# Gate and up weights loaded in blocks of 32 by 32 and turned on VectorE

## The chip, the core and the metric

One core of one Trainium2 chip. The metric is the device time of one execution in microseconds; the kernel before took 1469.0 us, the median of 3 runs (1468.91 to 1469.15). A core has TensorE (PE, matrix products; PEld is its weight load), VectorE (DVE), ScalarE (ACT), GpSimd (POOL) and SyncE (SP, which only issues transfers here). Each engine works through its own instructions in order.

## The reference

A gated block of cross-attention and a gated feed-forward network, all in f32: x is 4 x 1024 x 512, ctx 4 x 64 x 512, 16 heads of 64. The three weights of the feed-forward part are first rounded to 4-bit levels in blocks of 32 along their inner dimension; activations are rounded to 16-bit levels with one scale for a whole tensor. Cut to what the change touches:

```
def lpbq_dequant(w):                      # w is O x I
    wb = w.reshape(O, I // 32, 32)
    s  = max(max(|wb|, axis=-1) / 7, 1e-12)
    return (clip(round(wb / s), -8, 7) * s).reshape(O, I)

x    = act_qdq(layernorm(x))                           # 16-bit levels, one scale
up   = act_qdq(x @ lpbq_dequant(w_up).T)               # w_up:   1536 x 512
gate = act_qdq(x @ lpbq_dequant(w_gate).T)             # w_gate: 1536 x 512
gate = act_qdq(gate * fixed_qdq_u16(sigmoid(gate)))
out  = act_qdq(gate * up) @ lpbq_dequant(w_down).T     # w_down: 512 x 1536
```

The two products contract over the 512 inputs, and TensorE contracts over partitions. So gate's and up's weights are wanted with the inputs on partitions, while in DRAM a row is one output, and the blocks of 32 lie along the row.

## The kernel before

The stages follow each other: preparation of the attention's matrices (to about 80 us of the span); attention, a loop over 16 pairs of token tiles (L735, q is the pair, one iteration about 28 us); the gate stage from 561 us, 24 units (the loop at L981), each of 7 products of blocks in the manner of Strassen, 4 matmuls of 128x512 each; the up stage with 24 such units; and the down stage. PE's order is written out by hand (manual_schedule, L818 for the gate and up stages); the other engines are ordered by a planner that goes by priorities, except where keep_in_program_order or high_priority says otherwise.

The 512 inputs are HC = 4 groups of 128. A weight of 1536 outputs is IC = 12 chunks of 128 rows. One chunk goes through these steps:

- `dequantized` (L216): one load of 256 KB on SP's queue (L218), 128 rows of 2 KB. On DVE the largest magnitude of each block (L221), its scale (L224) and reciprocal (L226), the product rounded to int16 (L229), and the product with the scale (L230).
- `turned_chunk` (L243) and `turned` (L232): four PE transposes of 128x128 into PSUM (L235), and one ACT copy of 128x512 out of it (L237) into wgT or wuT. Those hold four chunks each, with inputs on partitions.

`slot()` gives the large buffers, 20 in turn of 128 x 2048 f32 each; a load into a slot waits for what last used it.

Where it stands: in attention, iterations q = 1 to 12 load and round one gate chunk each (`made_ready`, L790), chunks 4 to 11 first, then 0 to 3. The groups 4 to 7 and 8 to 11 are stored by POOL as rows in wg_d (L793), since the slots are needed, and come back at q = 13 and 14 (L800). At q = 13, 14 and 15 PE turns four chunks each ahead of the attention's last product (L769). At q = 13 and 14 the first four chunks of up are loaded and rounded too (`early_up`); PE turns them in the tail of attention (L808, L811). The rest of up, chunks 4 to 11, is loaded and rounded in units 0 to 7 of the gate stage and turned one unit later (L981 to L998). From unit 8 the 12 chunks of the down weight are rounded, one a unit; they are turned later by PE as well (`down_turned`, L264, which stays). `weight_sums` (L279) makes the sums of weight blocks that the seven products need, on DVE: two for gate at the end of attention, the other in the first unit, and those of up from unit 12.

Lines that the prediction speaks of: in attention, scores L570, maximum L594 and L604, exponentials L606, the normalisation L611 and L612, transposes of the weights L627, the product with the values L661, its addition to the tokens (xg) L669; the normalised tokens L692 (xm), their transposes L700 and copies L702; sums over a batch's matrices L381 to L386; loads of token groups L302 and of batch matrices (mb, vb) L710. In the units: the matmul L839 and the copy out of PSUM L855 (raw_gate).

Of the kernel before, what the change touches and what calls it, by code (L numbers as in the profile page):

```python
# [7 lines left out]
F32 = mybir.dt.float32  # L8
I16 = mybir.dt.int16
# [3 lines left out]
ALU = mybir.AluOpType  # L13
AX = mybir.AxisListType
PSUM = bass.MemoryType.PSUM
DRAM = bass.MemoryType.DRAM

P = 128
# [9 lines left out]
def kernel(  # L28
# [40 lines left out]
    nc = tc.nc  # L69
    B, S, H = x.shape  # L70
# [5 lines left out]
    T = B * S  # L76
    NT = T // P
    TPB = S // P
    HC = H // P
    HP = NH // 2  # L80
    IC = I // P
# [7 lines left out]
    QB = 32  # L89
    NQB = H // QB  # L90
# [8 lines left out]
    BL = 32  # L99
    UPE = 4  # L100
    SOON = 150
    NQ = NT // 2
# [6 lines left out]
    dram = ctx.enter_context(tc.tile_pool(name="dram", bufs=1, space=DRAM))  # L109
    big = ctx.enter_context(tc.tile_pool(name="big", bufs=NS))  # L110

    def slot(shape, name, dtype=F32):

        return big.tile(shape, dtype, name=name, tag="s8")
# [6 lines left out]
        out=cmask, in_=cmask, compare_op=ALU.is_ge, fill=-10000.0, base=0,  # L121
# [27 lines left out]
    off2 = const.tile([P, NT], F32, name="off2")  # L149

    x1_d = [dram.tile([P, H], F32, name=f"x1_d{t}") for t in range(NT)]
    wg_d = [dram.tile([P, 4, H], F32, name=f"wg_d{k}") for k in range(2)]
    xh_d = [dram.tile([P, HC, TB], F32, name=f"xh_d{g}") for g in range(NG - 2)]
    m_d, vwo_d = (
        {b: [dram.tile([P, HC, H], F32, name=f"{n}_d{b}_{k}") for k in range(2)] for b in range(2, B)}
# [57 lines left out]
            nc.vector.tensor_scalar(inv, inv, unit, None, ALU.mult)  # L213
        return s, inv

    def dequantized(pool, src, w, name, in_order=False):  # L216

        nc.sync.dma_start(out=w, in_=src)  # L218
        wb = w.rearrange("p (n k) -> p n k", k=QB)
        am = pool.tile([P, NQB], F32, name=f"wam_{name}", tag="wam")  # L220
        ins = nc.vector.tensor_reduce(am, wb, AX.X, ALU.max, apply_absolute_value=True)  # L221
        if in_order:
            tc.keep_in_program_order(ins)
        nc.vector.tensor_scalar(am, am, 1.0 / W_QMAX, 1e-12, ALU.mult, ALU.max)  # L224
        inv = pool.tile([P, NQB], F32, name=f"winv_{name}", tag="winv")
        nc.vector.reciprocal(inv, am)  # L226
        shape = [P, NQB, QB]
        wi = pool.tile(shape, I16, name=f"wi_{name}", tag="wi", bufs=1)
        nc.vector.tensor_tensor(wi, wb, inv.unsqueeze(2).to_broadcast(shape), ALU.mult)  # L229
        nc.vector.tensor_tensor(wb, wi, am.unsqueeze(2).to_broadcast(shape), ALU.mult)  # L230

    def turned(ps, w, dst):  # L232

        for j in range(4):
            nc.tensor.transpose(ps[:, j, :], w[:, j * P : (j + 1) * P], ident)  # L235
        with tc.high_priority(SOON):
            nc.scalar.copy(dst, ps)  # L237

    wgT, wuT, wd, wdT, up_chunks = [], [], [], [], []

    def turned_chunk(psp, w, oc, into, name):  # L243

        if oc % 4 == 0:
            into.append(slot([P, HC, 4 * P], f"w{name}T{oc // 4}"))
        cols = slice((oc % 4) * P, (oc % 4 + 1) * P)
        ps = psp.tile([P, 4, P], F32, name=f"wps_{name}{oc}", tag="tr")
        turned(ps, w, into[-1][:, :, cols])

    def up_chunk(psp, w):
        oc = len(up_chunks)
        up_chunks.append(oc)
        turned_chunk(psp, w, oc, wuT, "u")

    def down_chunk(pool, k):
        if k % 4 == 0:
# [70 lines left out]
    pa = pools.enter_context(tc.tile_pool(name="pa", bufs=2))  # L328
# [222 lines left out]
    with tc.tile_pool(name="ps_s", bufs=1, space=PSUM) as ps_s, tc.tile_pool(  # L551
# [157 lines left out]
                parts[k] = slot([P, HC, H], f"{name}_{k}")  # L709
                nc.sync.dma_start(out=parts[k], in_=src[k])  # L710

        sg_t, ag, early_up, gate_raw = [], [], [], []
        last = NT - GRP
        norm_of(pa, first_norm(*range(1, 5)), "a1")

# [1 line left out]
            if q < NQ:  # L717
                left[q] = score_left(q, two)

        def made_ready(ws, n, src, name, first=0, in_order=False):  # L720

            oc = (len(ws) + first) % n
            if oc % 4 == 0:
                made_in.append(slot([P, min(4, n - oc), H], f"w_{name}{oc}"))
            w = made_in[-1][:, oc % 4, :]
            dequantized(pa, src[oc * P : (oc + 1) * P, :], w, f"{name}{oc}", in_order)
            ws.append(w)

        made_in = []
        two = centred(1)  # L730
        ahead = scores(0, {3: lambda: next_left(1)})
        softmax(0, ahead)
# [2 lines left out]
        for q in range(NQ):  # L735
# [28 lines left out]
            if q % 2 == 1 and q // 2 + 2 < NG:  # L764
                load_group(q // 2 + 2)
                if q // 2 + 2 > 4:
                    group_stats(pa, q // 2 + 2, xg[q // 2 + 2])

            j = q - (NQ - IC // 4)  # L769
            if j >= 0:  # L770
                for oc in range(4 * j, 4 * j + 4):
                    turned_chunk(ps_tr, gate_raw[oc], oc, wgT, "g")
            if q + 1 == NQ:
                for p in range(UPB - 2):
                    ag.append(weight_sums(wgT, sg_t, p, "g"))
# [12 lines left out]
                norm_of(pa, parts, f"b{g}")  # L788

            if 0 < q <= IC:  # L790
                made_ready(gate_raw, IC, w_gate, "g", 4, q < 4)
                if q % 4 == 0 and q < IC:
                    nc.gpsimd.dma_start(out=wg_d[q // 4 - 1], in_=made_in[-1])  # L793
                if q == IC:
                    gate_raw = [*gate_raw[-4:], *gate_raw[:-4]]
            elif q > IC:
                k = q - IC - 1
                if k < 2:
                    w4 = slot([P, 4, H], f"wg_{k}")
                    nc.sync.dma_start(out=w4, in_=wg_d[k])  # L800
                    gate_raw[4 * k + 4 : 4 * k + 8] = [w4[:, i, :] for i in range(4)]
                for _ in range(2 if k < 2 else 0):
                    made_ready(early_up, UPE, w_up, "eu")
        renormed(last)
        renormed(last + 1)
        norm_of(pa, [second_norm(slice(last + 2, NT))], "c2")
        for w in early_up[:-1]:
            up_chunk(ps_tr, w)  # L808
        renormed(NT - 2)
        renormed(NT - 1)  # L810
        up_chunk(ps_tr, early_up[-1])  # L811
    pools.close()

    s_x, inv_x = act_scale(over_all([am_x], "x"), None, "x")

    with tc.tile_pool(name="praw", bufs=RAW) as praw, tc.tile_pool(
# [79 lines left out]


        au, su_t = [], []
        with tc.tile_pool(name="pb", bufs=2) as pb, tc.tile_pool(
            name="ps_tr2", bufs=2, space=PSUM  # L900
        ) as ps_tr:
            def on_dve(tb, h):
                v = xT[tb][:, h, :]
                nc.vector.tensor_scalar(v, v, inv_x, MAGIC, ALU.mult, ALU.add)
# [71 lines left out]


            pairs = [NTB // 2 - 1, *range(NTB // 2 - 1)]
            w4 = [slot([P, 4, H], "w_u4")]
            ready = []  # L980
            for at, v in enumerate(tp * UPB + p for tp in pairs for p in range(UPB)):  # L981
                if at % UPB == 0:
                    b = token_side(v // UPB)
                    for p in range(len(ag), UPB):
                        ag.append(weight_sums(wgT, sg_t, p, "g"))
                    if at + UPB < NV:
                        load_normed(pairs[at // UPB + 1])
                interleaved(unit_steps(v, ag[v % UPB], b, "gate", gate_sum, gate_done))
                if at < IC - UPE:
                    oc = UPE + at  # L990
                    if at == 4:
                        w4.append(slot([P, 4, H], "w_u8"))
                    w = w4[-1][:, at % 4, :]
                    dequantized(pb, w_up[oc * P : (oc + 1) * P, :], w, f"u{oc}")
                    ready.append(w)
                if len(ready) > 1 or at >= IC - UPE and ready:
                    up_chunk(ps_tr, ready.pop(0))
                if at >= IC - UPE and at - (IC - UPE) < IC:  # L998
                    down_chunk(pb, at - (IC - UPE))
                if 0 <= at - IC < UPB:  # L1000
                    au.append(weight_sums(wuT, su_t, at - IC, "u"))
# [503 lines left out]
```

## Time and profile before

| | |
|---|---|
| runs shown, median | 1469.0 us |
| profiled execution, its own time | 1467.07 us |
| its span (first to last instruction) | 1465.3 us |
| PE's granted clock over the span | 0.995 |
| L235 transposes of gate and up | 96, 273 ns each at the median |
| L237 copies of wgT | 12, 6.2 us, 620 ns each |
| L237 copies of wuT | 12, 6.9 us, 594 ns each |
| L221, L229, L230 of gate, one chunk | 667, 686 and 685 ns |
| transposes on DVE (L396, 128x32) | 1, 211 ns |
| chunk loads (L218) of gate | 12, median 427 ns on SP |

One execution is profiled, on its own, so a sum made from its rows is compared with its own 1467.07 us. The runs shown lie 1.9 us above it. Busy time of an engine counts its instructions; short ones overlap in part, so the place that a row of them takes on its engine is read from the start of the first to the start of what follows.

### The profile page before, as it was taken

How to read it: one execution, taken by the hardware profiler on the slowest of the kernel's cores; microseconds unless marked ns; L12 is line 12 of the kernel's file. 1: busy time of each engine (PE TensorE's matmuls, PEld its weight loads, DVE VectorE, ACT ScalarE, POOL GpSimd, SP SyncE). 2: the span in 40 equal slices, each digit the busy share in tenths (PEclk: the TensorE clock that was granted, in tenths of full speed). 3: DMA queues.
4: the chain of work that ended last, by engine and by line, in shares of the span. 5: the costliest groups of instructions: out<-in, count | busy, mean ns of one | idle time of the engine just before them, and what ended most of it. 6: DMA issues, size and time to landing. Idle time of an engine off the chain costs nothing. (4 is left out here: it accounts for less than half of the span.)

```text
span 1465.3 us, 15463 instructions
## 1 busy us (share of the span) xinstructions
PE 1417.2 (97%) x5040; PEld 869.3 (59%) x5040; DVE 1128.0 (77%) x2059; ACT 693.4 (47%) x1746; POOL 96.6 (7%) x191
## 2 busy tenths in 40 slices
PE   8898999999999998999999999999999899999999
PEld 6545766766676674444444444444444448888887
DVE  2976887977988779899956569988888897666632
ACT  2645867767678673111000049977776532222200
POOL 0100000000000001000000000000000101111110
PEclk9999999999999999999999999999999999999999
DMA  9630231431312133664322439958557475554321
GB/s 330 244 130 15 72 115 72 159 129 58 130 47 110 46 130 158 236 223 187 129 86 102 157 127 345 373 216 316 212 210 267 164 282 174 187 187 172 143 72 43
DMA packets 74168, 240.12 MB, mean 164 GB/s; under 512 B 7396, under 2 KB 7652, under 8 KB 68068
## 3 DMA queue, kind: packets, MB, share of 16 engines
q1 hardware_dynamic: 48612, 137.39, 26.8%
q0 software_dynamic: 18560, 76.56, 13.4%
q10 hardware_dynamic: 6912, 25.17, 4.3%
q8 instruction: 39, 0.64, 0.2%
q14 instruction: 45, 0.37, 0.1%
HBM read 130.03 MB, written 109.05 MB: 163 GB/s over the span
## 5 line engine op out<-in xcount | busy, mean ns | idle before, releaser
L606 ACT ACTIVATE e<-e,mx 128x64 f32<-128x64 f32 x480 | 159.7, 339 | 2.2 <-DVE mx L604 2.1
L839 PE MATMUL pqup<-t,wuT 128*128 128x512 f32 x192 | 92.3, 603 | 5.2 <-DVE raw_up L860 2.6
L606 ACT ACTIVATION_READ_ACCUMULATOR e<-e,mx 128x1 f32 x480 | 92.3, 192 | 0.0
L839 PE MATMUL pqgate<-t,wgT 128*128 128x512 f32 x192 | 90.2, 592 | 0.0
L855 ACT COPY raw_gate<-ppgate 128x512 f32<-128x512 f32 x24 | 14.0, 585 | 145.5 <-PE ppgate L839 145.5
L1372 PE MATMUL ep<-wdT,upe 128*128 128x256 f32 x336 | 77.1, 379 | 0.0
L1298 ACT ACTIVATE uie<-upe,inv_up 128x1024 int16<-128x1024 f32 x48 | 53.8, 1145 | 45.8 <-DVE upe L1302 28.7
L661 PE MATMUL oq<-t,eT 128*128 128x256 f32 x256 | 63.7, 393 | 12.0 <-DVE xg L669 8.1
L1372 PE MATMUL eq<-tw,upe 128*128 128x256 f32 x312 | 72.4, 379 | 0.0
L1372 PEld LDWEIGHTS ep<-wdT,upe 128*128 128x128 f32 x336 | 63.8, 190 | 9.1 <-issue 0.5
L1071 ACT ACTIVATE gi<-gt,inv_gate 128x1024 int16<-128x1024 f32 x48 | 54.9, 1143 | 30.3 <-DVE q L1081 30.0
L839 PEld LDWEIGHTS pqup<-t,wuT 128*128 128x128 f32 x192 | 34.7, 189 | 57.0 <-issue 29.7
L839 PE MATMUL ppgate<-xh,wgT 128*128 128x512 f32 x144 | 67.7, 592 | 0.0
L839 PE MATMUL ppup<-xu,wuT 128*128 128x512 f32 x144 | 67.7, 592 | 0.0
L1372 PEld LDWEIGHTS eq<-tw,upe 128*128 128x128 f32 x312 | 59.3, 190 | 8.1
L839 PEld LDWEIGHTS pqgate<-t,wgT 128*128 128x128 f32 x192 | 36.3, 190 | 46.1 <-issue 37.9
L1302 DVE SCALAR_TENSOR_TENSOR upe<-uie,inv_o,gse 128x1024 f32<-128x1024 int16 (+1 forms) x50 | 60.4, 1231 | 3.3 <-ACT uie L1298 3.0
L661 PEld LDWEIGHTS oq<-t,eT 128*128 128x128 f32 x256 | 49.4, 195 | 21.9 <-DVE xg L669 11.0
L570 PE MATMUL sq<-t,xs 128*128 128x512 f32 x128 | 60.3, 593 | 0.0
L629 ACT COPY eT<-ps_e 128x512 f32<-128x512 f32 x64 | 34.3, 588 | 53.5 <-PE ps_e L627 53.5
L967 DVE TENSOR_REDUCE am_gate<-raw_gate 128x1 f32<-128x1024 f32 x48 | 58.2, 1213 | 0.9
L1103 ACT ACTIVATE ar<-raw_up 128x1024 f32<-128x1024 f32 x46 | 48.2, 1047 | 19.1 <-DVE raw_up L1029 19.1
(353 smaller groups left out, 3141.2 us busy)
## 6 DMA issues: line engine op xcount, KB each, us to landing
gate_d<-raw_gate ACTq DMA_DIRECT2D x48, 512.0 KB, 2.6
gt<-gate_d SPq DMA_DIRECT2D x48, 512.0 KB, 4.8
upe<-up_d SPq DMA_DIRECT2D x24, 1024.0 KB, 5.9
up_d<-raw_up POOLq DMA_DIRECT2D x46, 512.0 KB, 3.5
gse<-gsi_d SPq DMA_DIRECT2D x24, 512.0 KB, 4.6
gsi_d<-q SPq DMA_DIRECT2D x44, 256.0 KB, 4.0
xg<-in_x_dram SPq DMA_DIRECT2D x8, 1024.0 KB, 5.2
x_d<-xg POOLq DMA_DIRECT2D x32, 256.0 KB, 2.3
```

The costliest lines, as they stand in the source:

```text
L570: nc.tensor.matmul(bank[at], a[k][:, h, :], b[k][:, h, :], start=start and h == 0, stop=h == HC // 2 - 1, skip_group_check=True,)
L606: nc.scalar.activation(ei[:, h, :], ei[:, h, :], AF.Exp, bias=mx[:, h : h + 1], accum_out=sm[:, h : h + 1],)
L629: nc.scalar.copy(eT[:, 2 * i + k], ps)
L661: nc.tensor.matmul(bank[at], a[k][:, h, :], b[k][:, h, :], start=start and h == 0, stop=h == HP // 2 - 1, skip_group_check=True,)
L839: nc.tensor.matmul(bank[at], a[k][:, h, :], b[k][:, h, :], start=start and h == 0, stop=h == HC // 2 - 1, skip_group_check=True,)
L855: nc.scalar.copy(r0[:, 0, :], bank["pp"])
L967: nc.vector.tensor_reduce(am_gate[:, u : u + 1], rf, AX.X, ALU.max, apply_absolute_value=True)
L1071: nc.scalar.activation(gi, g, AF.Copy, scale=inv_g)
L1103: nc.scalar.activation(ar, raw[u], AF.Abs)
L1298: nc.scalar.activation(ui, up[:, i, :], AF.Copy, scale=inv_u)
L1302: ins = nc.vector.scalar_tensor_tensor(o[:, i, w], ui[:, w], c_o, gs[:, i, w], ALU.mult, ALU.mult)
L1372: nc.tensor.matmul(bank[at], a[u // 2][k][:, u % 2, q % 2, :], w_of[u // 2][k][:, u % 2, :], start=start and u == 0, stop=u == UPB - 1, sk ...
```

## The change

A chunk of gate or up is loaded straight into its place in wgT or wuT, by 16 loads: one for each 32 inputs within a group (a) and each group of inputs (c). Each writes 32 partitions with 4 x 32 elements, in pieces of 32 elements (128 bytes). Partition a·32 + o then holds outputs, column block b holds 32 inputs a·32 to a·32 + 31 of output b·32 + o. Blocks of 32 still lie along a row, so the rounding (`levels`) works on it as before, in a view of four dimensions. Then one DVE transpose in place turns each 32 by 32 block, which puts inputs on partitions and outputs along the row. No PE transposes and no ACT copies are left for gate and up; the down weight keeps them.

wg_d keeps turned groups, and both come back at q = 13. Up's chunks 0 to 3 are made at q = 13 and 14 as before; its chunks 4 to 11 are made in units 2 to 9 of the gate stage (before: 0 to 7), with their first instruction kept in program order. The PSUM buffers of the gate stage's transposes (ps_tr2) go.

```diff
-    wg_d = [dram.tile([P, 4, H], F32, name=f"wg_d{k}") for k in range(2)]
+    wg_d = [dram.tile([P, HC, 4 * P], F32, name=f"wg_d{k}") for k in range(2)]
...
-    def turned_chunk(psp, w, oc, into, name):
+    def turned_chunk(pool, src, oc, into, name, in_order=False):
         if oc % 4 == 0:
-            into.append(slot([P, HC, 4 * P], f"w{name}T{oc // 4}"))
-        cols = slice((oc % 4) * P, (oc % 4 + 1) * P)
-        ps = psp.tile([P, 4, P], F32, name=f"wps_{name}{oc}", tag="tr")
-        turned(ps, w, into[-1][:, :, cols])
+            into[oc // 4] = slot([P, HC, 4 * P], f"w{name}T{oc // 4}")
+        w = into[oc // 4][:, :, (oc % 4) * P : (oc % 4 + 1) * P]
+        blocks = w.rearrange("p c (b k) -> p c b k", k=BL)
+        rows = src[oc * P : (oc + 1) * P, :].rearrange("(b o) (c a k) -> a o c b k", o=BL, k=BL, c=HC)
+        for a in range(P // BL):
+            for c in range(HC):
+                nc.sync.dma_start(out=blocks[a * BL : (a + 1) * BL, c], in_=rows[a, :, c])
+        levels(pool, blocks, [P, HC, P // BL, QB], f"{name}{oc}", in_order)
+        nc.vector.transpose(w, w)
...
-            j = q - (NQ - IC // 4)
-            if j >= 0:
-                for oc in range(4 * j, 4 * j + 4):
-                    turned_chunk(ps_tr, gate_raw[oc], oc, wgT, "g")
...
             if 0 < q <= IC:
-                made_ready(gate_raw, IC, w_gate, "g", 4, q < 4)
-                if q % 4 == 0 and q < IC:
-                    nc.gpsimd.dma_start(out=wg_d[q // 4 - 1], in_=made_in[-1])
+                oc = (q + 3) % IC
+                turned_chunk(pa, w_gate, oc, wgT, "g", q < 4)
+                if oc > 3 and oc % 4 == 3:
+                    nc.gpsimd.dma_start(out=wg_d[oc // 4 - 1], in_=wgT[oc // 4])
...
             elif q > IC:
...
+                for j in (1, 2) if k == 1 else ():
+                    wgT[j] = slot([P, HC, 4 * P], f"wgTb{j}")
+                    nc.sync.dma_start(out=wgT[j], in_=wg_d[j - 1])
+                if k < 3:
+                    for oc in range(2 * k - 2, 2 * k):
+                        turned_chunk(pa, w_up, oc, wuT, "u")
...
-        for w in early_up[:-1]:
-            up_chunk(ps_tr, w)
         renormed(NT - 2)
         renormed(NT - 1)
-        up_chunk(ps_tr, early_up[-1])
...
-                if at < IC - UPE:
-                    oc = UPE + at
...
-                    dequantized(pb, w_up[oc * P : (oc + 1) * P, :], w, f"u{oc}")
-                    ready.append(w)
-                if len(ready) > 1 or at >= IC - UPE and ready:
-                    up_chunk(ps_tr, ready.pop(0))
+                if 1 < at < IC - UPE + 2:
+                    oc = UPE + at - 2
+                    turned_chunk(pb, w_up, oc, wuT, "u", True)
```

`levels` is the DVE part of the old `dequantized`, with the shape handed in:

```diff
+    def levels(pool, w, shape, name, in_order=False):
...
+        ins = nc.vector.tensor_reduce(am_b, w, AX.X, ALU.max, apply_absolute_value=True)
...
+        nc.vector.tensor_tensor(wi, w, inv_b.unsqueeze(len(shape) - 1).to_broadcast(shape), ALU.mult)
+        nc.vector.tensor_tensor(w, wi, am_b.unsqueeze(len(shape) - 1).to_broadcast(shape), ALU.mult)
```

## The prediction

> **What bounds the kernel now.** The first part of the page says which engine is full, the second where.
>
> ```profile
> PE 1417.2 (97%) x5040; PEld 869.3 (59%) x5040; DVE 1128.0 (77%) x2059; ACT 693.4 (47%) x1746; POOL 96.6 (7%) x191
> ...
> PE   8898999999999998999999999999999899999999
> ...
> DVE  2976887977988779899956569988888897666632
> ...
> PEclk9999999999999999999999999999999999999999
> DMA  9630231431312133664322439958557475554321
> ```
>
> The reader is to see that TensorE (PE) is at nine tenths in nearly every slice at full clock, so an instruction taken off PE is worth its place on PE, unless another engine then keeps PE waiting. The engine to suspect is VectorE (DVE): 77% over the span, nine tenths in slices 17 to 20. One slice is 36.6 us; the edit lies in slices 3 to 19. So the second view is that of stretches of 50 us (columns: window; its length; busy PE, PEld, DVE, ACT, POOL with instructions; clock; DMA share; GB/s).
>
> ```profile
> 450.00:500.00 50.00, 49.68 (x223) 35.27 (x222) 35.96 (x76) 39.26 (x154) 1.61 (x3) 1.00 0.14 53
> 500.00:550.00 50.00, 48.32 (x233) 36.98 (x232) 41.18 (x100) 33.00 (x111) 2.16 (x4) 1.00 0.30 106
> 550.00:600.00 50.00, 44.62 (x134) 22.78 (x133) 48.71 (x109) 13.06 (x24) 5.73 (x11) 0.97 0.47 177
> 600.00:650.00 50.00, 50.00 (x130) 22.89 (x129) 40.02 (x76) 7.03 (x12) 2.12 (x4) 1.00 0.70 253
> 650.00:700.00 50.00, 50.00 (x124) 22.51 (x123) 49.73 (x107) 5.85 (x10) 2.28 (x4) 1.00 0.41 158
> ```
>
> Attention ends near 551; from 561 the gate stage runs. In 600 to 700 PE has no gap, though DVE is full in the second half: the gate stage is PE's, with a DVE that just keeps up. From 550 to 600 PE loses 5.4 us, and DVE has 1.3 us free there: the turn between the stages is DVE's. The third view, PE's timeline, shows what the removed transposes really hold (start, length, instructions, idle before and its releaser).
>
> ```profile
> 489.28 0.60 PE L235 MATMUL wps_g<-ident,w_g 128*128 128x128 f32 x4
> 490.20 1.62 PE L235 MATMUL wps_g<-ident,w_g 128*128 128x128 f32 x12 [0.32 <-ACT xT L702]
> 491.65 1.89 PE L661 MATMUL opn<-vb,eT 128*128 128x256 f32 x8
> ...
> 520.08 1.63 PE L235 MATMUL wps_g<-ident,wg 128*128 128x128 f32 x12 [1.10 <-ACT xT L702]
> 521.55 1.89 PE L661 MATMUL opn<-vb,eT 128*128 128x256 f32 x8
> ...
> 536.63 2.11 PE L235 MATMUL wps_g<-ident,wg 128*128 128x128 f32 x16
> 538.58 1.89 PE L661 MATMUL opn<-vb,eT 128*128 128x256 f32 x8
> ...
> 557.10 1.94 PE L700 MATMUL ps_xm<-ident,xm 128*128 128x128 f32 x8 [3.30 <-DVE xm L692]
> 558.83 1.06 PE L235 MATMUL wps_u<-ident,w_eu 128*128 128x128 f32 x4
> 561.08 1.96 PE L839 MATMUL ppgate<-xT,wgT 128*128 128x512 f32 x4 [1.19 <-DVE xT L905]
> ...
> 581.19 0.60 PE L235 MATMUL wps_u<-ident,w_u 128*128 128x128 f32 x4
> 581.63 1.88 PE L839 MATMUL ppgate<-xT,wgT 128*128 128x512 f32 x4
> ```
>
> **Removed from PE: 96 transposes.** The groups give one as 273 ns; 96 of those would be 26 us. But they are pipelined: 16 in a row stand between 536.63 and 538.58, 0.12 us each. So a place is read from start to start of what follows. Gate: 491.65 − 489.28 = 2.37; 521.55 − 518.38 (where its first four start) = 3.17, with a wait of 1.10 in it; 1.95: together 7.5 us. Up, first four chunks: they stand in the tail of attention, where PE waits for DVE (3.30 and 1.19 us): 0. Up, other eight: 8 × 0.44 (581.19 to 581.63) = 3.5 us. Gross 11.0 us. The rule against this edit is in the Trainium skill, VectorE: DVE Perf Modes, section Rules for kernel authors: a full 128x128 transpose belongs on TensorE if PSUM is an acceptable target. TensorE: Matmul & The Clock Gate, Part 4, gives about 275 ns for one in a kernel's context; the row (273) agrees as a duration, but as a place on PE it would make the edit worth 26 us, and the timeline 11. I take the timeline.
>
> **Removed from ACT:** 24 copies of 128x512 out of PSUM, 6.2 + 6.9 = 13.1 us; ACT is free half of the time in these stretches. Two fours of them (2.04 and 2.06 us, at 490.5 and 520.4) stand ahead of exponentials; without them the last softmax could end up to 4 us earlier, if DVE follows.
>
> **Added to DVE: 24 transposes of 128x512.** The trace has one of 128x32, 211 ns, beside a scan of that size with 202. Other 128x512 instructions take 667 to 686 (reduce 667, the two multiplies 686 and 685) and follow each other at about 0.60. On DVE's timeline 128x256 instructions stand 0.34 us apart, 128x512 ones 0.60, so 480 more elements cost 0.49: 0.70 us. The skill's VectorE page, The three transpose paths, gives 311 ns for 128x128 in bf16, so four make 1.24 us. I take 0.6 to 0.7, because a row of the same operation and rows of the same size agree on it; ends 0.5 and 1.24. Sum 24 × 0.7 = 16.8 us of DVE (ends 12 and 30), 0.7 a chunk. The other five instructions of a chunk are the same ones in another order of elements: no change. A chunk now arrives by 16 loads, and its reduce may wait on several of them; such a wait costs DVE 21 ns in the trace, at most 8 × 21 = 0.17 us a chunk.
>
> **Added to SP and DMA: 384 loads of 16 KB for 24 of 256 KB.** Four chunk loads stand on SP in 1.77 us (at 95.25), a load of this kind has median 427 ns, so 0.43 each. A chunk takes 16 × 0.43 = 6.9 us of SP, a batch of four 27.5, all 165 us. Landing was 2.6/3.2/10.7 us (least, median, most). Each load has 128 pieces as before, but of 128 bytes and not 2 KB: 49,152 pieces, where the page has 74,168 packets in all. The nearest row for the number of pieces is the old load: 128 pieces at 0.43. The skill's DMA: Bandwidth & Descriptors, section Bandwidth, speaks against it: transfers under 64 KB are descriptor-dominated and should be batched to 1 MiB. Its fit, 2.0 us + 16 KB / 436e3 = 2.04, makes 33 us a chunk one after another; with eight in flight, 4.1, less than SP's issue. So I take issue, 6.9, and 33 as the far end. What is queued behind on SP: the second batch (from 228.9) has issued two chunks when it meets the loads of vb, which wait for their buffers until 264.3; its 28 loads behind them end at 276.8. The last two chunks then land near 273 and 280; by the changed order DVE wants them near 298 and 303. The token group behind is first used after 300. The third batch (from 330) meets vb at 372 to 380; its last two land near 390 and 397, wanted near 400 and 437; the next token group, loaded by 395, is used at 436. Up's first four start at 439.7 and are wanted after 504; the others start near 515 and 548, wanted a unit each from 585 and 634. The smallest cover is 10 us over 16 loads, so 0; gone, if a load costs three times its issue, see D.
>
> **Moved: up's chunks 4 to 11 from units 0–7 to 2–9 of the gate stage, in order.** A unit is 7 products × 1.717 = 12.02 us of PE. I count DVE's work for each unit from its instructions in the changed order times their spacing (0.60 for 128x512, 1.15 for 128x1024): before at most 14.6 (units 5 to 12), after 12 to 16 (units 2 to 13). The running excess over 12.02 reaches about 13 us before, with no gap on PE, and about 12.5 after, since units 0 and 1 get lighter. So nothing is lost; but the cover is thin, and each microsecond of DVE beyond it costs PE one.
>
> **The turn of the stages** decides about the 7.5 us. In attention PE's older gaps (324.7, 383.7, 442.6, up to 2.9 us) are at batch sums ahead of which no added instruction stands. In the last iteration, however, two early chunks (2.75 us each plus 0.6 of transpose) now lie between the last softmax and its normalisation, and three more weight sums. DVE then has 19.2 us of work without a gap from about 513.5, so the normalisation ends at 532.7 and not 534.7: of the 2.37 + 3.17 = 5.5 us only 2.0 are kept. In the last attention product a wait for sums is in both; I get its end at 548.1 and not 551.4. **3.2 us kept of 7.5**, and DVE is late next. From there to the first gate product (9.7 us) the chain is one of DVE instructions, the same ones before and after: 0.
>
> **Sum.** 3.2 + 3.5 = 6.7 us. On the profiled execution's 1467.07 (span 1465.3): 1460.4. The runs shown have median 1469.0, 1.9 above it; same difference: **1462.3**.
>
> **Rivals.**
> - A, the sum above: 1459 to 1465. Chance 0.40.
> - B, PE's whole 11 us and 1 from a shorter ACT queue: 1457. For it: DVE has 9 us free in 500 to 550. Against: that free time lies before the last softmax, not after. 0.17.
> - C, DVE eats the gain: transposes at 1.24 us make 0.5 × 24 = 13 us more DVE; where DVE is full (units 2 to 13, eight chunks) that is 4 us, and at the turn, with two chunks and waits, 2 to 3. Then 1466 to 1472. 0.18.
> - D, the small loads arrive late. Place: the last chunks of the second and third batch, behind vb's wait on SP. Price: at 1.5 us a load they land near 310 and 407, 7 and 5 us after they are wanted; DVE, which works in order, stands at the chunk's reduce, with the softmax that PE needs queued behind it: 1474. At the fit's 2.04 one after another, the chunks, vb and a token group are 20 to 30 us late in each of three places: about 1530. It decides from some 1.4 us a load. For it: a sixteenth of the bytes in a piece; DMA share already 0.70 in 600 to 650. Against: pieces per load are unchanged, and SP issues no faster. 0.13.
> - E, DVE's backlog in units 2 to 13 passes what PE's PSUM banks cover, since the eight chunks are now held in order among the unit's sums: 12 units × up to 1 us, less the gain: 1472 to 1476. For it: DVE 49.73 of 50. 0.12.
>
> **The numbers.** A difference of 0.2% is 2.9 us, about what a measurement can tell from none. Faster: A and B, 0.57, plus little of C: 0.58. Same: most of C, 0.17. Slower: D, E and C's end, 0.25. The range takes A, B, C and E: 1456 to 1476; left out are most of D and the far ends.
>
> **What would show it.** PE's instructions fall by 96 and its busy time by some 26 (durations overlap). The stretch 650 to 700 shows PE at 50: no backlog; a gap before a PE product with releaser DVE raw_gate would be E. The in-place transpose at 0.6 to 0.7 us. Batches on SP of 27 to 28 us and landing under 5; above 10, or idle DVE before the chunk's reduce, is D. The last attention product ending near 548 of the span is A, 544 B. Wrong above all if DVE is idle behind a load, or if the last softmax is later than before.

## The result and the profile after

No change that can be told: the changed kernel has a median of 1469.84 us (1467.24 to 1471.67) beside 1468.87 us (1466.79 to 1470.74) for the kernel before on the same chip, 12 runs each, ratio 1.0004 [0.9995, 1.0013]. The profiled execution has a span of 1465.5 us, where before it was 1465.3. The forecast was 1462.3.

The page of the changed kernel (busy time, the slices, the packets):

```profile
PE 1410.6 (96%) x4944; PEld 860.6 (59%) x4944; DVE 1143.7 (78%) x2083; ACT 681.7 (47%) x1722; POOL 97.7 (7%) x191
...
PE   8898999999999988899999999999999899999999
...
DVE  2976988997998788799976569888888897666632
...
DMA packets 126011, 240.17 MB, mean 164 GB/s; under 512 B 62308, under 2 KB 62564, under 8 KB 119908
```

The 96 transposes are off PE and DVE has its 24 turns. In slices 15 to 17 (513 to 623 us) PE has three eights where it had one: PE has less to do there and the same time goes by. The stretches of 50 us, to be laid beside those shown of before (length; busy PE, PEld, DVE, ACT, POOL; clock; DMA share; GB/s):

```profile
500.00:550.00 50.00, 43.58 (x192) 33.72 (x190) 44.79 (x113) 28.68 (x94) 2.17 (x4) 0.93 0.23 63
550.00:600.00 50.00, 40.63 (x93) 17.78 (x94) 37.49 (x74) 8.78 (x15) 6.46 (x10) 0.91 0.63 230
600.00:650.00 50.00, 50.00 (x113) 21.93 (x112) 45.68 (x83) 4.38 (x8) 3.20 (x6) 0.96 0.71 241
650.00:700.00 50.00, 50.00 (x117) 21.93 (x116) 49.75 (x105) 5.00 (x9) 0.00 (x0) 1.00 0.34 136
```

From 550 to 600 PE is busy 4 us less than before and DVE 11 us less (37.49 for 48.71). Neither engine fills the stretch, so what each of them waits for has to be looked up. The timelines settle where the gain went, by four landmarks on PE: the first attention product, the product after the last batch sum (442.55 before, 438.79 after), the first product of the gate stage, and that of the up stage. The first row below is left out of comparisons in what follows: in the twelve profiled executions of this document the first attention product starts between 81.8 and 84.3 us, ahead of every edited instruction, which moves spans by as much.

| us | before | after | difference |
|---|---|---|---|
| start to first attention product | 82.06 | 81.77 | −0.29 |
| to the product after the last batch sum | 360.49 | 357.02 | −3.47 |
| from there to the first gate product ("the turn") | 118.53 | 117.43 | −1.10 |
| gate stage, to the first up product | 287.99 | 292.86 | +4.87 |
| to the end | 616.23 | 616.42 | +0.19 |

Attention and the turn brought 4.6 us, and the gate stage gave them back. Inside the gate stage the loss is one place. PE of the changed kernel (start, length, instructions, idle before and its releaser):

```profile
592.71 1.88 PE L829 MATMUL pngate<-t,sg 128*128 128x512 f32 x4
599.06 3.78 PE L829 MATMUL pqgate<-t,wgTb 128*128 128x512 f32 x4 [4.48 <-DVE raw_gate L855]
602.64 2.69 PE L829 MATMUL ppgate<-xT,wgTb 128*128 128x512 f32 x4
605.17 1.88 PE L829 MATMUL pngate<-xT,sg 128*128 128x512 f32 x4
```

The same products in the kernel before:

```profile
597.52 1.88 PE L839 MATMUL pngate<-t,sg 128*128 128x512 f32 x4
599.23 1.88 PE L839 MATMUL pqgate<-t,wgT 128*128 128x512 f32 x4
...
602.67 1.88 PE L839 MATMUL pngate<-xT,sg 128*128 128x512 f32 x4
```

The product at 592.71 is the 21st of the stage and stands 4.81 us ahead of its counterpart (597.52). The 22nd, at 599.06, is only 0.17 ahead (599.23), and the 24th, at 605.17, is 2.50 behind (602.67): PE idles 4.48 us, and then two products take 3.58 and 2.53 us from start to start where they take 1.72. The clock in the stretches around it shows why (same columns as above):

```profile
590.00:595.00 5.00, 4.58 (x11) 1.50 (x9) 3.23 (x7) 0.59 (x1) 0.00 (x0) 1.00 0.82 260
595.00:600.00 5.00, 0.94 (x1) 0.50 (x2) 2.35 (x4) 0.00 (x0) 0.00 (x0) 0.74 0.83 302
600.00:605.00 5.00, 5.00 (x8) 2.07 (x7) 3.60 (x8) 0.00 (x0) 0.00 (x0) 0.57 0.26 67
```

So one wait costs 4.64 + 2.67 = 7.3 us. After it, PE gains 0.44 at each of the six places where a chunk's four transposes used to stand, and by 668.69 is 0.13 ahead again.

PE's releaser is a copy on DVE, and DVE's timeline shows what held that copy:

```profile
592.68 0.69 DVE L232 TENSOR_TENSOR wuT<-wi_u,wam_u 128x512 f32<-128x512 int16 x1
597.65 0.75 DVE L892 TENSOR_SCALAR xh<-xh,inv_x 128x1024 f32<-128x1024 f32 x1 [4.29 <-DMA xh<-xh_d]
598.32 0.68 DVE L855 TENSOR_TENSOR raw_gate<-pqgate,raw_gate 128x512 f32<-128x512 f32 x1
```

The rounding of a token group (`on_dve`, L892) waits for the group's load; the copy that frees PE's bank of PSUM (the memory that PE writes its products to) stands behind it, as DVE works in order. This token group (of pair 1) belongs to unit 12, some 108 us later. In the kernel before, its rounding stood at 637.43; in the changed kernel, where up's chunks are held in program order and stand two units later, the planner put it into unit 3. And the load was late, as SP's timeline shows:

```profile
505.12 85.64 SPq L261 DMA_DIRECT2D wuT<-in_L_ffn_w_up_dram  x64
590.85 0.95 SPq L963 DMA_DIRECT2D xh<-xh_d  x2
592.02 33.40 SPq L261 DMA_DIRECT2D wuT<-in_L_ffn_w_up_dram  x48
```

The 64 loads of four up chunks stand ahead of it and hold SP 85.64 us, where 64 × 0.43 = 27.5 were reckoned. The view of SP's waits from 500 to 640 (total, times, longest) has the rest, first of the changed kernel, then of the kernel before:

```profile
SPq L261 <- DMA gate_d<-raw_gate: 56.8, 3, 53.6
```

```profile
SPq L975 <- DMA gate_d<-raw_gate: 59.0, 3, 53.7
```

A load on SP waits 53.6 us for a store of gate's raw results, which ACT issues and which has no data in common with it. What ties them is the completion semaphore: the counter that a transfer raises as it lands, and that must be free before the next transfer which was given it can start. The traces hold the number of each transfer's semaphore. SP's and ACT's transfers take eight of them in turn here (101, 102 and 104 to 109), across both queues; POOL's have eight of their own (111 to 118). Number 109 belongs to the first gate store and then to the 43rd of the 64 small loads. That store comes after the first unit: it is issued at 573.13 and has landed at 579.68, and the load starts at 579.69.

In the kernel before, the same kind of wait, as long, fell on a token group's load itself: semaphore 107 was held by the third gate store, which landed at 594.19, and the load was issued at 594.27. Its user came at 637.43, so the wait cost nothing. The change did not make the wait. It put up's loads and the token group behind it, and the group's user earlier.

### The profile page after: what moved, and what is told of

The parts are those of the page before. It is cut to its first block, busy times and chain, and to the rows that moved or that the text cites. A ratio compares the mean times of both kernels' runs of the same rounds, so it can differ in the third digit from the quotient of the medians.

```text
span 1465.5 us, 15707 instructions
## 1 busy us (share of the span) xinstructions
PE 1410.6 (96%) x4944; PEld 860.6 (59%) x4944; DVE 1143.7 (78%) x2083; ACT 681.7 (47%) x1722; POOL 97.7 (7%) x191
## 3 DMA queue, kind: packets, MB, share of 16 engines
q1 hardware_dynamic: 100452, 137.41, 28.1%
## 5 line engine op out<-in xcount | busy, mean ns | idle before, releaser
L845 ACT COPY raw_gate<-ppgate 128x512 f32<-128x512 f32 x24 | 14.1, 586 | 151.3 <-PE ppgate L829 144.6
L829 PE MATMUL pqgate<-t,wgTb 128*128 128x512 f32 x128 | 62.2, 609 | 4.5 <-DVE raw_gate L855 4.5
L837 ACT COPY raw_gate<-ppgate 128x512 f32<-128x512 f32 x24 | 14.1, 586 | 108.5 <-PE ppgate L829 62.9
L1061 DVE SCALAR_TENSOR_TENSOR q<-gi,inv_gs,si 128x1024 int16<-128x1024 int16 x44 | 56.3, 1282 | 2.1 <-ACT si L1054 1.0
```

Of the source, the lines that this page charges most:

```text
L829: nc.tensor.matmul(bank[at], a[k][:, h, :], b[k][:, h, :], start=start and h == 0, stop=h == HC // 2 - 1, skip_group_check=True,)
L1061: nc.vector.scalar_tensor_tensor(gsi[u], gi, c_gs, si, ALU.mult, ALU.mult)
```

## The experiments

What is measured of all of them: the median, the ratio to the kernel before on the same chip [95% interval], and three of the stretches between landmarks, read from PE's timeline of each kernel's one profiled execution (us).

| kernel | median | ratio | to the last sum | turn | gate stage |
|---|---|---|---|---|---|
| before | 1468.87 | | 360.49 | 118.53 | 287.99 |
| after | 1469.84 | 1.0004 [0.9995, 1.0013] | 357.02 | 117.43 | 292.86 |
| gate_only | 1460.72 | 0.9946 [0.9926, 0.9966] | 357.01 | 112.49 | 289.49 |
| up_only | 1474.86 | 1.0043 [1.0028, 1.0057] | 360.42 | 120.00 | 293.41 |
| xh_first | 1469.31 | 1.0004 [0.9992, 1.0015] | 357.00 | 117.49 | 295.50 |
| pinned | 1469.13 | 1.0002 [0.9990, 1.0013] | 357.01 | 117.55 | 294.03 |
| one_load | 1465.44 | 0.9974 [0.9966, 0.9981] | 359.90 | 118.99 | 285.23 |
| no_turn | 1469.90 | 1.0007 [1.0000, 1.0014] | 357.41 | 117.88 | 292.10 |
| up_pool | 1460.00 | 0.9947 [0.9929, 0.9964] | 357.01 | 117.46 | 285.71 |
| stores_pool | 1463.68 | 0.9964 [0.9952, 0.9976] | 357.03 | 117.51 | 285.77 |
| mixed_pool | 1458.06 | 0.9924 [0.9905, 0.9943] | 357.02 | 112.51 | 286.69 |
| all_late | 1458.11 | 0.9927 [0.9904, 0.9951] | 357.89 | 111.99 | 288.60 |

### xh_first: the token group's load ahead of up's

```diff
-                    nc.sync.dma_start(out=xT[g], in_=xh_d[g])
+                    with tc.high_priority(2000):
+                        nc.sync.dma_start(out=xT[g], in_=xh_d[g])
```

> The changed kernel with the loads of normed tokens (xh) given a higher priority, so that xh2 and xh3 stand on SP ahead of 63 of the 64 small loads of up's chunks 4 to 7; nothing else is edited. Theory (DVE stands 4.3 us for xh2, which is queued behind small loads; PE then loses 4.5 us and another 2.7 us to a lowered clock): DVE has no wait on xh in unit 3, PE no gap at unit 3, the gate stage's products are 7 to 7.7 us earlier than in the kernel before, ratio to before 0.995 (1461 to 1462). Rival 1 (DVE has too much to do in units 2 to 9): the gap at unit 3 comes back as a wait for DVE raw_gate within a unit or two, ratio 0.998 to 1.001. Rival 2 (small loads as such hold the token loads up, by sharing the DMA engines): xh2 lands late though issued early, ratio 1.000.

The load now stands ahead of 63 of the 64 small loads, and the stall at 597 is gone, yet the gate stage is longer still (295.50). PE and then DVE:

```profile
595.53 3.20 PE L829 MATMUL pqgate<-t,wgTb 128*128 128x512 f32 x4 [2.55 <-DVE raw_gate L850]
...
636.83 3.53 PE L829 MATMUL pqgate<-t,wgTb 128*128 128x512 f32 x4 [3.28 <-DVE raw_gate L850]
```

```profile
592.33 0.69 DVE L952 TENSOR_REDUCE tops_all<-raw_gate 128x1 f32<-128x512 f32 x1 [4.22 <-ACT raw_gate L845]
...
633.09 0.75 DVE L892 TENSOR_SCALAR xh<-xh,inv_x 128x1024 f32<-128x1024 f32 x1 [4.42 <-DMA xh<-xh_d]
```

At 633 the next token group is late in the same way. At 592 DVE waits for a copy on ACT, and ACT's timeline has it behind a store:

```profile
591.35 0.33 ACTq L958 DMA_DIRECT2D gate_d<-raw_gate  x1
591.71 0.59 ACT L845 COPY raw_gate<-ppgate 128x512 f32<-128x512 f32 x1 [10.12 <-PE pqgate L829]
```

ACT had been idle 10.12 us. The coupling works in the other direction as well: this store's data were complete at 588.1, and it stands until a small load that has the same semaphore (108) lands at 591.25, with ACT's copies behind it. The ratio is that of rival 1, but its cause is not seen: at both places DVE waits (4.22 and 4.42 us) and has no excess of work. Moving one late load forward moves the wait to the next user.

### pinned: the early user held back

The rounding of token pair 1 is called at unit 9 with its four DVE instructions in program order.

```diff
-                nc.vector.tensor_scalar(v, v, inv_x, MAGIC, ALU.mult, ALU.add)
+                ins = nc.vector.tensor_scalar(v, v, inv_x, MAGIC, ALU.mult, ALU.add)
+                if in_order:
+                    tc.keep_in_program_order(ins)
...
+                if at == 9:
+                    b_early = token_side(pairs[2])
```

> The changed kernel with the rounding of token pair 1 (xh2, xh3) on DVE kept in the order of the program at unit 9, where the planner had put it into unit 3; the loads stay where they are on SP. Theory (it takes both, a late load and an instruction moved ahead that waits for it): no wait for xh2 in unit 3, so 7 us come back, ratio 0.995 to 0.997, unless the next pair's rounding (xh4, loaded from 636), which the planner may now move ahead, waits in its place. Rival 1 (DVE overloaded in units 2 to 9): a gap of PE remains, and more work in unit 9 makes it worse, ratio 1.000 to 1.003.

The stall at 597 is gone here too, and again the stage is not shorter (294.03). PE and DVE of this kernel:

```profile
607.25 1.98 PE L829 MATMUL pqgate<-t,wgTb 128*128 128x512 f32 x4 [1.11 <-DVE raw_gate L850]
...
647.86 2.83 PE L829 MATMUL pqgate<-t,wgT 128*128 128x512 f32 x3 [3.87 <-DVE raw_gate L850]
```

```profile
643.45 0.75 DVE L892 TENSOR_SCALAR xh<-xh,inv_x 128x1024 f32<-128x1024 f32 x1 [4.10 <-DMA xh<-xh_d]
```

The 64 loads still hold SP 85.94 us, and the next pair, issued at 635.66, is waited for at 643.45, which is the exception that the expectation named. So the early rounding is where the wait showed, not what makes it: that the planner's reordering is the cause falls with this run.

### gate_only and up_only: each half of the change alone

In gate_only up's weights go the way of before, by `made_ready`, `up_chunk` and PE; in up_only gate's do.

```diff
-                if k < 3:
-                    for oc in range(2 * k - 2, 2 * k):
-                        turned_chunk(pa, w_up, oc, wuT, "u")
+                for _ in range(2 if k < 3 else 0):
+                    made_ready(early_up, UPE, w_up, "eu")
...
+        for w in early_up[:-1]:
+            up_chunk(ps_tr, w)
...
-                if 1 < at < IC - UPE + 2:
-                    oc = UPE + at - 2
-                    turned_chunk(pb, w_up, oc, wuT, "u", True)
+                if at < IC - UPE:
+                    oc = UPE + at
```

> The kernel before with the change made for gate alone: gate's chunks by 16 loads and turned on DVE, up's chunks as before (one load each, PE transposes and ACT copies, units 0 to 7). Theory: the lead of PE at the first gate product is as in the changed kernel, 4 to 5 us, and stays, since SP has no small loads in front of xh2: ratio 0.997 (1464 to 1465). Rival 1 (DVE gives the gain back in any case): lead 0 to 2 us at the end of the gate stage, ratio 0.999 to 1.001.

And for up_only:

```diff
-                oc = (q + 3) % IC
-                turned_chunk(pa, w_gate, oc, wgT, "g", q < 4)
...
+                made_ready(gate_raw, IC, w_gate, "g", 4, q < 4)
...
+                for oc in range(4 * j, 4 * j + 4):
+                    turned_chunk(ps_tr, gate_raw[oc], oc, wgT, "g")
```

> The kernel before with the change made for up alone: up's chunks by 16 loads and turned on DVE, chunks 4 to 11 in units 2 to 9; gate as before with PE transposes. Theory: no lead at the first gate product, 3.5 us from the eight places of transposes on PE in the gate stage, and the gap at unit 3 with its slower clock (7 us), since the small loads stand ahead of xh2 as in the changed kernel: ratio 1.002 (1471 to 1473). Rival (the stall needs gate's part too, as PE is then ahead of the loads): no gap, ratio 0.998.

Gate alone is worth 0.54%, up alone costs 0.43%, and together they give nothing. Two things come apart. The gate stage is long only with up's loads (293.41 in up_only, with a gap of 3.86 at 605.33). And the turn is 4.9 us shorter with gate alone (112.49) than with both (117.43). For the turn, first PE of gate_only, then of the changed kernel. Counted from each one's first attention product (83.61 and 81.77), the three products come 2.89, 4.86 and 4.95 us earlier in gate_only:

```profile
529.37 1.06 PE L661 MATMUL ps_e<-ident,e 128*128 128x128 f32 x8 [1.74 <-DVE mv L343]
549.17 1.94 PE L734 MATMUL ps_xm<-ident,xm 128*128 128x128 f32 x8 [3.44 <-DVE xm L726]
553.11 3.75 PE L867 MATMUL ppgate<-xT,wgT 128*128 128x512 f32 x4 [1.15 <-ACT wuT L255]
```

```profile
530.42 1.94 PE L636 MATMUL ps_e<-ident,e 128*128 128x128 f32 x8 [4.47 <-DVE r_c L177]
552.19 1.33 PE L709 MATMUL ps_xm<-ident,xm 128*128 128x128 f32 x8 [4.14 <-DVE xm L701]
556.22 3.75 PE L829 MATMUL ppgate<-xT,wgT 128*128 128x512 f32 x4 [2.71 <-ACT xi L898]
```

DVE of the changed kernel between the last two normalisations (L621) that these transposes of `e` wait for:

```profile
523.13 1.18 DVE L621 TENSOR_TENSOR e<-e,rs 128x1024 f32<-128x1024 f32 x1
...
528.52 0.63 DVE L232 TENSOR_TENSOR wuT<-wi_u,wam_u 128x512 f32<-128x512 int16 x1
529.06 1.21 DVE L621 TENSOR_TENSOR e<-e,rs 128x1024 f32<-128x1024 f32 x1
...
530.27 0.69 DVE L263 STREAM_TRANSPOSE wuT<-wuT 128x512 f32<-128x512 f32 x1
```

(PE's row names r_c, a short instruction that ends at 530.35, beside the second normalisation's 530.27.) An up chunk's rounding stands among them and ahead of the second one, and another chunk's ahead of the first; in gate_only the last early chunk has its last step at 507.63, ahead of the last softmax. What is saved on PE at the turn is then waited for on DVE.

### one_load and no_turn: the loads' number, or DVE's turn

```diff
-        rows = src[oc * P : (oc + 1) * P, :].rearrange("(b o) (c a k) -> a o c b k", o=BL, k=BL, c=HC)
-        for a in range(P // BL):
-            for c in range(HC):
-                nc.sync.dma_start(out=blocks[a * BL : (a + 1) * BL, c], in_=rows[a, :, c])
+        nc.sync.dma_start(
+            out=w, in_=src[oc * P : (oc + 1) * P, :].rearrange("p (c n) -> p c n", c=HC)
+        )
```

> The changed kernel with each chunk of gate and up loaded by one load of 256 KB in place of 16 of 16 KB; rounding and turning on DVE stay. It leaves out the placing of the 32 by 32 blocks (rows lie as in DRAM), so the weights are other ones, of the same shapes. Theory (the gain is given back by what 384 small loads do: they fill SP's queue ahead of the token loads, tie ACT's stores and SP's loads together by the shared completion semaphores, and make the planner place up's early chunks later on DVE): the first gate product 7 to 9 us earlier than before, counted from the first attention product, no gap of PE in the gate stage, ratio 0.992 to 0.994 (1457 to 1460). Rival (the in-place turns and the chunks held in order on DVE are the cost): still a gap at unit 3 or later, ratio 0.998 or more.

```diff
-        nc.vector.transpose(w, w)
```

> The changed kernel without the 24 in-place transposes on DVE; it leaves out the turning within blocks, so the weights are other ones; the small loads stay. Theory (small loads): the gaps of the gate stage stay, the turn of the stages gains at most 1 to 2 us (two transposes of 0.6 and some waiting), ratio 0.998 to 1.001. Rival (DVE's added 17 us are the cost): ratio 0.995 or less.

Without the 24 DVE turns nothing moves: 1469.90, the gate stage 292.10. With one load a chunk, and the turns in place, the gate stage takes 285.23, which is 7.6 less than in the changed kernel and 2.8 less than before. So in the gate stage it is the loads and not the work added to DVE. The rest of the expectation for one_load failed: its ratio is 0.9974, between those of the theory and the rival, because attention shows none of the 3.5 us gain. DVE's order there is another, and the run does not separate why.

### up_pool: up's loads on another queue

Up's chunks 4 to 11 are loaded by POOL; the loads are the same.

```diff
-                    turned_chunk(pb, w_up, oc, wuT, "u", True)
+                    turned_chunk(pb, w_up, oc, wuT, "u", True, nc.gpsimd)
```

> The changed kernel with the small loads of up's chunks 4 to 11 issued by POOL in place of SP, so that they have neither SP's queue nor the completion semaphores of SP and ACT; all else as in the changed kernel. Theory: no wait of DVE on xh and no wait of ACT's stores on small loads in the gate stage; the gate stage is 3 to 4 us shorter than before, the turn as in the changed kernel (4.6 us), ratio 0.994 to 0.996. Rival (the small pieces slow the other transfers on the DMA engines themselves): xh still lands late, ratio 0.999 or more. A third way: POOL issues so slowly that chunks come late at units 2 to 9, a gap with DVE standing at a chunk's reduce.

Gate stage 285.71, ratio 0.9947; the stage is 2.3 us shorter than before, where 3 to 4 were expected. 128 loads of 16 KB, of the same small pieces, do no harm where no token group and no store is tied to them. But this run takes away two things at once: the place ahead of the token groups on SP, and the shared semaphores.

### stores_pool: all small loads left on SP, only the stores moved

```diff
-                nc.scalar.dma_start(out=gate_d[u], in_=rf)
+                nc.gpsimd.dma_start(out=gate_d[u], in_=rf)
```

> The changed kernel with one line altered: the stores of the gate stage's results (gate_d) go out on POOL's queue in place of ACT's. All 384 small loads stay on SP, as do the token loads behind them. Theory (it is the completion semaphores that SP's loads and ACT's stores share, and not the number or size of the loads): SP no longer stands 53.6 us at the 43rd of up's second 64 loads, its loads are out by some 540, the token loads xh2 and xh3 land before 560, DVE doesn't stand for them, and the gate stage is as short as with the loads on POOL (some 286 us from its first product to the up stage's first): ratio 0.994 to 0.996. Rival (SP's queue of small loads itself is too slow): xh2 still lands after 590 and the gap at unit 3 stays, ratio 1.000.

This tells them apart. All 384 small loads are on SP in the same order, ahead of the same token groups. SP's timeline:

```profile
507.19 31.72 SPq L261 DMA_DIRECT2D wuT<-in_L_ffn_w_up_dram  x64
539.01 0.85 SPq L963 DMA_DIRECT2D xh<-xh_d  x2
540.08 29.51 SPq L261 DMA_DIRECT2D wuT<-in_L_ffn_w_up_dram  x48
```

The same 64 loads take 31.72 us and not 85.64: the difference, 53.9, is the one wait. The token group is issued at 539.01, and the gate stage takes 285.77, as in up_pool. One line is worth 7.1 us of gate stage. That a load waited for an unrelated store is thus shown, and so is its price; that the shared semaphore is the tie is read from its numbers in the traces, and was not tried with more than eight of them. Of the whole kernel the line brings less than up_pool does: the median is 6.2 us below the changed kernel's, and 3.7 above up_pool's. The two profiled executions differ by 1.9 ahead of the first attention product and by 3.0 behind the gate stage; whether the stores on POOL cost something there was not separated.

### mixed_pool and all_late: towards a better kernel

mixed_pool loads and turns gate as changed, leaves up's first four chunks to PE as before, and turns up's other eight on DVE with loads on POOL:

```diff
-                if k < 3:
-                    for oc in range(2 * k - 2, 2 * k):
-                        turned_chunk(pa, w_up, oc, wuT, "u")
+                for _ in range(2 if k < 3 else 0):
+                    made_ready(early_up, UPE, w_up, "eu")
...
-                    turned_chunk(pb, w_up, oc, wuT, "u", True)
+                    gate_chunk(pb, w_up, oc, wuT, "u", True, nc.gpsimd)
```

> Gate's chunks as in the changed kernel; up's first four chunks as before (one load, PE transposes in the tail of attention); up's chunks 4 to 11 turned on DVE in units 2 to 9 with their small loads issued by POOL. Theory: the turn as in the run with gate alone (9.5 us gained), and 3 us more from PE's eight places in the gate stage: ratio 0.991 to 0.993 (1455 to 1458). Rival (DVE overloaded in units 2 to 9): gaps of PE in the gate stage, ratio 0.995 or more, not better than gate alone.

all_late makes all twelve up chunks in units 0 to 11, with loads on POOL:

```diff
-                if k < 3:
-                    for oc in range(2 * k - 2, 2 * k):
-                        turned_chunk(pa, w_up, oc, wuT, "u")
...
-                if 1 < at < IC - UPE + 2:
-                    oc = UPE + at - 2
-                    turned_chunk(pb, w_up, oc, wuT, "u", True)
+                if at < IC:
+                    turned_chunk(pb, w_up, at, wuT, "u", True, nc.gpsimd)
```

> The changed kernel with up's small loads on POOL and with all twelve of up's chunks in units 0 to 11 of the gate stage, so that none of up's work is left in attention. Theory (the turn of the stages is dear in the changed kernel because up's early chunks lie on DVE in the last softmax): from the first attention product to the first gate product as with gate alone or less, 467 to 470 us (474.5 in the changed kernel), and the ratio 0.991 to 0.993 if DVE keeps up in units 0 to 12. Rival (the turn is set by the weight sums and not by the early chunks): 473 to 475 us there. A third way: DVE is overloaded in units 8 to 12, where four chunks of up and four of down coincide, and PE shows gaps of some us there, ratio 0.995 or more.

Both keep the short turn (112.51 and 111.99) and most of the gate stage, and both beat both kernels: 1458.06, ratio 0.9924, and 1458.11, ratio 0.9927. (Against gate_only, 1460.72, the intervals overlap.) all_late shows that the early chunks are what made the turn dear, and not the weight sums. It gives back 2.9 us in the gate stage against up_pool: DVE is full there (49.93 of 50 in 650 to 700) and PE has a gap of 1.13 at 652.61.

## Why the prediction was wrong

**The step that failed** is the cost of the added loads, "the smallest cover is 10 us over 16 loads, so 0". The issue was right: 430 ns at the median. The landing, 1.6/1.8/8.3 us (least, median, most), stayed under the 5 that the working allowed at the median, and not at the most. But cover was reckoned for the chunks that the loads bring, and from issue times alone. What was queued behind up's loads in the gate stage, the token groups, was not asked for in this batch, though it was for the two of attention; and a wait of 53.7 us on SP for a gate store stood in the trace of before and has no place in the working. In the changed kernel such a wait, 53.6 us, stopped up's loads and the token group behind them; DVE then stood 4.29 us for the group and PE 4.48, and two products ran slow. The term put at 0 measured 7.3 us.

- **PE's gross 11.0 us** was right where it can be read: eight places of 0.44 in the gate stage, 3.5 in all. Without the wait the stage is 2.3 (up_pool, 285.71) or 2.8 (one_load) shorter than before, so most of the 3.5 is kept.
- **The turn**, 3.2 kept of 7.5, measured 1.1. That early up chunks between the last softmax and its normalisation would eat it was right in kind and too small: gate_only and all_late reach the first gate product 4.9 and 4.6 us sooner, counted from the first attention product, than the changed kernel and up_pool.
- **Attention's older gaps**, where nothing was expected, gave 3.47. In the trace of before and then of after, at the same product:

```profile
324.74 3.65 PE L661 MATMUL oq<-t,eT 128*128 128x256 f32 x8 [2.86 <-DVE xg L669]
328.22 1.89 PE L661 MATMUL opn<-vwo,eT 128*128 128x256 f32 x8
```

```profile
323.05 1.99 PE L670 MATMUL oq<-t,eT 128*128 128x256 f32 x8 [1.80 <-DVE xg L678]
324.88 1.89 PE L670 MATMUL opn<-vwo,eT 128*128 128x256 f32 x8
```

The gap is 1.06 shorter, and the product behind it 1.66, since it no longer runs at half speed: 2.7 of the 3.47. It was not foreseen, and it is luck for the sum. The sign said to show A, a last attention product ending near 548, came (547.0 for 551.4 before) mostly by it. Why DVE is earlier there stays open; it shows in gate_only and no_turn and not in up_only or one_load.

- **The sum**: −3.47, −1.10 and +4.87 make +0.3, and with −0.29 and +0.19 at the ends the +0.2 of the two spans. The forecast had −3.2 for attention and turn and −3.5 for the gate stage. The gate stage is 8.4 off its term (4.87 + 3.5): 7.3 of the wait, 0.7 of a slower first product behind a longer gap at the turn (3.55 us to the next product for 2.84), and some 0.4 in small steps. The rest is 1.4 on the good side (4.57 for 3.2).
- **DVE's turn** was right: 24 at 0.70 us, as the groups show.

```profile
L263 DVE STREAM_TRANSPOSE wgT<-wgT 128x512 f32<-128x512 f32 x12 | 8.4, 699 | 0.2
...
L263 DVE STREAM_TRANSPOSE wuT<-wuT 128x512 f32<-128x512 f32 x12 | 8.3, 695 | 0.1
```

Rival C falls with it, and with no_turn: nothing comes back when the turns go. That the measured time lies in C's range (1466 to 1472) is chance. Rival E falls with up_pool, where the same eight chunks are held in order and the stage is shorter than before; and 650 to 700 shows PE at 50.00 with DVE at 49.75.

- **Rival D** had the mechanism, a late load and DVE standing in order in front of it, but in attention, for the chunks themselves, and by the price of a load. The place was the gate stage, the victim another load, and the price one wait.
- **The sign said to show E**, a gap before a product with releaser raw_gate, appeared at 599.06 and was not E: the copy was held by a late load and not by a backlog. Only DVE's own timeline told these apart. The sign that the prediction put above all, DVE idle behind a load, is the one that came true.
- **PE's busy time** fell by 6.6 us and not 26: places and not durations count, and products after gaps took longer.
- **A reading** of the first view is off by a slice: DVE's nines stand in slices 16 and 18 to 20, and 17 has an eight. Nothing rests on it.

## What to carry to other kernels

Before adding many transfers to a queue, look in the trace of before for every long wait of that queue, also of one that costs nothing now, and ask what will stand behind it after the change. If a transfer waits for another with which it shares no data, move one of the two to another queue before moving priorities: here one line brought 7.1 us of gate stage, and two changes of order brought none. And when work is taken off a full engine, put what replaces it where its new engine has room: the early chunks cost 4.9 us at the turn, and 2.9 when they were made in the gate stage, where DVE is full as well.

## What was not expected of the hardware

- **The clock after a gap.** In the traces the granted clock is full, or half for 3.41 us or a multiple of it, on a fixed grid of such steps. Before, the gap of 2.86 us at 324.74 lies in one step (2.83 of its 3.41 us are idle), and the clock is half in the next, 324.71 to 328.13: the product takes 3.65 us for 1.99. The gap of 2.86 at 442.55 is cut by the edge at 440.77 into 1.08 and 1.78, and the clock stays full. In the twelve traces, between 20 and 1450 us, every step at full clock in which PE was idle for more than 2.0 us was followed by half clock (59 of them), and of all with less only one, with 1.98. So a gap of 2.86 can cost its own length or 1.7 us more, by where the grid falls. After 4.48 us the granted clock stands at 0.57 for the following 5 us, so the gap costs 60% on top of itself. The Trainium skill, TensorE: Matmul & The Clock Gate, Part 1, gives half rate after at least one idle window of about 3.4 us; the steps agree with its length, but here a window that was idle for 2.0 us was enough.
- **Small loads are cheap.** 16 KB in 128 pieces of 128 bytes land in 1.8 us at the median (the working's estimate, from the fit in the Trainium skill, DMA: Bandwidth & Descriptors, Anatomy of one DMA, which is for transfers issued by POOL, was 2.04) and hold SP 0.43. There are 52,000 more packets, and the share that the packets of SP's queue take of the DMA engines goes from 26.8% to 28.1%. With the stores out of the way the gate stage takes 285.77 us with all 384 small loads, and 285.23 with 24 large ones. What they use up is something else: sixteen completions a chunk, where there was one.
